# A Mamba layer on one core: roots and statistics moved to ScalarE, gates of two blocks in one instruction, and a new plan of parts

## The chip, the core and the metric

The kernel runs on one core of one Trainium2 chip. The core has five engines that run side by side, each taking its own instructions in order: TensorE (PE in the profile, with its weight loads shown as PEld), VectorE (DVE), ScalarE (ACT), GpSimd (POOL) and SyncE (SP), which here issues all DMA transfers. They meet through semaphores. SBUF is the working memory of 128 partitions; PSUM takes what PE computes[...]. The metric is the device time in microseconds of one execution, taken as the median of several runs.

## The reference, cut to what matters

The input x has 4 images of 384 channels and 64 x 64 pixels. Two layers follow each other, each with a group norm (32 groups of 12 channels) in front and the input added behind.

```python
# layer 0: a Mamba block over the L = 4096 pixels of each image
xn = (xs - mu) * rsqrt(var + 1e-5) * ln_w + ln_b        # over channels, of the group-normed x
xb, z = split(xn @ in_proj.T)                           # 768 and 768
xc = silu(conv4(xb) + conv_b)
dt, Bm, Cm = split(xc @ x_proj.T)                       # 24, 16, 16
dt = softplus(dt @ dt_w.T + dt_b)
h = exp(dt * A) * h + (dt * xc) * Bm                    # a scan over L, 768 x 16 states
y = sum_n(h * Cm) + xc * D
x1 = x + (y * silu(z)) @ out_proj.T
# layer 1: outlook attention on the group-normed x1, windows of 3 x 3, stride 2
out = x1 + proj(fold(softmax(attn(pool(g(x1)))) @ values(g(x1))))
```

The group norm in front of layer 1 needs mean and variance of x1 for each group of 12 channels, over all 4096 pixels of an image. All numbers are fp32.

## The kernel before, in words

**Tiling.** The pixels of each image are cut into 17 chunks of 241 (the first has 240 of its own and one column of zeros), 68 chunks in all. Channel 3p + cb lies in partition p, so a group of 12 channels is 4 partitions times NCB = 3 column blocks, and `blk12`, a matrix with blocks of 4 x 4, averages over a group on PE.

**The scan.** A chunk's 768 x 16 states are done in 12 steps, each a *unit* of two half-units (k = 0, 1) of 128 x 968 numbers. A step costs:
- `s_inputs` (L625) on POOL and `s_inputs2` (L640) on DVE: the products dt * x * B for one half each of the states, written into the tile h (five buffers, L137). The trace shows them as h<-dxr,bc and h<-dxr,bp.
- `s_decay` (L649) on ScalarE: eight ACTIVATEs exp(dt * A) into two PSUM tiles da, one per half (da<-dtr,aneg).
- `s_scan` (L661) on DVE: two scan instructions (h<-da,h).
- `s_outputs` (L671) on POOL: h times C in place (h<-h,bc).
- every second step `s_sum` (L676) on PE: 17 matmuls sum the states of two units into the PSUM tile y; then `s_gate` (L694) on DVE multiplies y by silu(z) (zs<-y,zs).
- two small copies on ScalarE, `s_carry` and `s_save`, that hand the last state on.

In step s of the main loop (L805) the engines are at different units: DVE scans unit s, ScalarE makes the decays of s + 1, POOL multiplies s - 1 by C and then makes the inputs of s + 2, PE sums s - 3 and s - 2, DVE gates s - 3.

**The parts.** All else of a chunk is cut into parts, functions that issue one or a few instructions. The dictionary `plan` (L506) says at which step, and at which of six places within the step (EARLY, READY, SCAN, POOL, MID, LATE), each part stands; the step is counted so that a chunk's units are scanned in steps 24 to 35, and a chunk begins every 12 steps. So a place at step 18 is met at step 6 of every twelve. `ends` (L540) is the same for the part behind the scan, counted from step 36. This hand-written order is final: the wrapper InOrder keeps each engine's instructions in the order of issue, so an instruction that waits holds everything behind it on its engine.
- `f_load` to `f_scale` (the layer norm): x in; mean by PE; center on DVE; square on ScalarE; variance by PE; `f_root` (L316) adds 1e-5 on DVE; `f_pow` (L321) raises to -0.5 on POOL (vs<-vs,mhalf); `f_rs` spreads it by PE; scale on DVE.
- `f_x`, `f_z`, `f_conv`, `f_silu`, `f_bc`, `f_xd`, `f_dt`: projections, convolution, silu (two table loads around it on ScalarE) and the small projections.
- `f_plog` (L482), `f_dtx` (L487): Ln(1 + exp) on ScalarE into PSUM (ps_lg), times xc on DVE (dtx), stored to DRAM by four DMAs; `f_log` does the same Ln into SBUF and stores it; `f_spread` loads B and C over the partitions; `f_b` makes PE's copy of B (bp).
- `e_load`, `e_project` (L710), `e_store` (L718): x again; out_proj plus x on PE, copied by ScalarE (xr<-ps_out); three bn_stats on DVE for the group norm of layer 1, and the store of x1.

All these PSUM results but y, da and bp share the pool `pmm` (L139) with two buffers: the third user waits until the first is read.

**Group norm.** `group_norm_coeffs` (L76) turns bn_stats into scale and bias; it runs in pieces between steps. The statistics of the next image's x are gathered on the way, two instructions per chunk (x_stat, L823) in 12 chunks of each of the first three images.

While the last chunks are scanned, the first tile of layer 1 begins (from L851). Layer 1 has its own loop and the change does not touch it.

Of the kernel before, what the change touches and what calls it, by code (L numbers as in the profile page):

```python
# [12 lines left out]
P = 128  # L13
# [59 lines left out]
        self.before = group[:-1]  # L73


def group_norm_coeffs(pe, ve, ae, gp, small, psum, blk12, mhalf, st, sc, bi):  # L76

    mv = small.tile([P, NCB, 2], F32, tag="mv", name="mv")  # L80
    neg = small.tile([P, 1], F32, tag="mg", name="neg")
    dev = small.tile([P, NCB], F32, tag="dev", name="dev")
    for cb in range(NCB):
        ve.bn_aggr(mv[:, cb, :], st[cb])
    yield False
    ps = psum.tile([P, 2, TM], F32, tag="mm", name="pm")
    for cb in range(NCB):
        pe.matmul(ps[:, 0, 0:1], blk12, mv[:, cb, 0:1], start=(cb == 0), stop=(cb == NCB - 1))
    yield True
    ae.mul(neg, ps[:, 0, 0:1], -1.0)  # L90
    ae.activation(dev, mv[:, :, 0], AF.Square, bias=neg)
    yield False
    ps = psum.tile([P, 2, TM], F32, tag="mm", name="pv")
    for cb in range(NCB):
        pe.matmul(ps[:, 0, 0:1], blk12, mv[:, cb, 1:2], start=(cb == 0), stop=False)
    for cb in range(NCB):
        pe.matmul(ps[:, 0, 0:1], blk12, dev[:, cb : cb + 1], start=False, stop=(cb == NCB - 1))
# [8 lines left out]
def mamba_layer(ctx, tc, x, w, x1, sc1, bi1, consts, behind):  # L106
# [13 lines left out]

    nc = tc.nc
    B, _, L = x.shape
    blk12, ident, eps, one = consts
    pe, ve, ae, gp, sp = (
        InOrder(tc, e) for e in (nc.tensor, nc.vector, nc.scalar, nc.gpsimd, nc.sync)
    )
# [19 lines left out]
        sp.dma_start(t, w[name])  # L146
        return t

    mhalf = wp.tile([P, 2], F32, tag="mhalf", name="mhalf")
    gp.memset(mhalf, -0.5)  # L150


# [163 lines left out]
    def f_root(c):  # L316
        n = c.spans[0][1]
        c.vs = front.tile([P, 2], F32, tag="vs", name="vs")
        ve.tensor_scalar_add(c.vs[:n, :], c.pv[:n, :, 0], 1e-5)

    def f_pow(c):  # L321
        n = c.spans[0][1]
        gp.tensor_tensor(c.vs[:n, :], c.vs[:n, :], mhalf[:n, :], ALU.pow)

    def f_rs(c):
        c.ps = pmm.tile([P, 2, TM], F32, tag="mm", name="ps_rs")
# [172 lines left out]
    def at(f, *args):  # L499
        def part(c):  # L500
            f(c, *args)

        part.f = f
        return part

    plan = {  # L506
        (-12, SCAN): [f_load],
        (-10, EARLY): [f_mean],
        (-10, READY): [f_center],
        (-9, LATE): [f_square],  # L510
        (-7, EARLY): [f_var],
        (-7, MID): [f_root],
        (-6, LATE): [f_pow],
        (-5, READY): [f_rs],
        (-5, SCAN): [f_scale],
        (6, LATE): [at(f_x, 0)],
        (8, EARLY): [at(f_z, 0)],
        (8, MID): [at(f_x, 1)],
        (9, POOL): [at(f_z, 1)],
        (9, LATE): [at(f_conv, 0)],  # L520
        (10, LATE): [at(f_z, 2)],
        (11, LATE): [at(f_x, 2)],
        (12, MID): [at(f_conv, 1)],
        (13, SCAN): [at(f_conv, 2)],
        (13, POOL): [at(f_silu, "xc", "zs")],
        (14, POOL): [f_bc],
        (15, EARLY): [f_xd],
        (16, READY): [at(f_dt, 0)],
        (16, SCAN): [at(f_dt, 1)],
        (16, MID): [at(f_dt, 2)],  # L530
        (17, READY): [at(f_plog, 0)],
        (17, MID): [at(f_dtx, 0)],
        (18, EARLY): [at(f_plog, 1)],
        (18, SCAN): [at(f_dtx, 1), at(f_plog, 2)],
        (19, EARLY): [at(f_dtx, 2)],
        (19, MID): [f_log, f_spread],
        (22, SCAN): [f_b],
    }
# [137 lines left out]
    def s_sum(u, u2):  # L676

        c, t = u.c, u.t
        y = py.tile([P, TM], F32, tag="y", name="y")
        pe.matmul(y[:, :t], ddiag[:, u.j, :], c.xc[:, u.j, :TM], start=True, stop=False, skip_group_check=True)  # L680
        for g in range(NG):
            for i in range(4):
                h4 = (u, u2)[i // 2].h4
                pe.matmul(
                    y[CG * i : CG * (i + 1), :t],
                    ssum,
                    h4[:, i % 2, g, :TM],
                    start=False,
                    stop=(g == NG - 1),
                    skip_group_check=True,  # L690
                )
        u2.y = y

    def s_gate(u):  # L694
        c, t = u.c, u.t
        ve.tensor_mul(c.zs[:, u.j, :t], u.y[:, :t], c.zs[:, u.j, :t])


    st1 = {}
# [10 lines left out]
    def e_project(c, cb):  # L710
        lo = c.lo
        po = pmm.tile([P, 2, TM], F32, tag="mm", name="ps_out")
        pe.matmul(po[:, 0, lo:], ident, c.xr[:, cb, lo:TM], start=True, stop=False)
        for j in range(NJ):
            pe.matmul(po[:, 0, lo:], wout[:, j, cb, :], c.zs[:, j, lo:TM], start=False, stop=(j == NJ - 1))
        ae.copy(c.xr[:, cb, lo:TM], po[:, 0, lo:])

    def e_store(c):  # L718
        if c.ci == 0:
            st1[c.b] = small.tile([P, NCB, NC, 6], F32, tag="st1", name="st1")  # L720
        for cb in range(NCB):
            ve.bn_stats(st1[c.b][:, cb, c.ci, :], c.xr[:, cb, c.lo : TM])
        sp.dma_start(e_tokens(c, x1), c.xr[:, :, c.lo : TM])
        if c.ci == NC - 1:
            b = c.b
            st = [st1[b][:, cb].rearrange("p a s -> p (a s)") for cb in range(NCB)]
            made = group_norm_coeffs(
                pe, ve, ae, gp, small, pmm, blk12, mhalf, st, sc1[:, b : b + 1], bi1[:, b : b + 1]
            )
            norms.append([made, False])  # L730

# [73 lines left out]
    for s in range(-4, NU * (len(chunks) + 2)):  # L805
        k, m = divmod(s, NU)
        if m % 2 == 0 and unit(s + 4) is not None:
            s_fetch(s + 4)
        parts(s, EARLY)
        if m % 4 == 3 or s >= NU * len(chunks):  # L810
            norm_part(False)

        if (u := unit(s + 1)) is not None:
            s_inputs2(u)
        if (u := unit(s - 3)) is not None and not u.first:
# [12 lines left out]
        for i in range(2):  # L828
            if (u := unit(s)) is not None:
                s_scan(u, i)  # L830
            if i == 1:
                parts(s, SCAN)
            if (u := unit(s + 1)) is not None:
                if i == 0:
                    s_carry(u)
                s_decay(u, i)
            if i == 0 and (u := unit(s - 1)) is not None:
                s_save(u)
        if (u := unit(s - 1)) is not None:
            s_outputs(u)  # L840
        norm_part(True)
        parts(s, POOL)
        if (u := unit(s + 2)) is not None:
            s_inputs(u)
        if (u := unit(s - 2)) is not None and not u.first:
            s_sum(unit(s - 3), u)
        parts(s, MID)
        parts(s, LATE)
        if s == front_end:
            fronts.close()  # L850
        if s >= front_end:  # L851
            over = das[0] if s >= NU * len(chunks) - 1 else None
            behind(lambda: pmm.tile([P, 2, TM], F32, tag="mm", name="psv").rearrange("p a b -> p (a b)"), over)
# [386 lines left out]
def layers(ctx, tc, w, out):  # L1240
# [5 lines left out]
    x1 = dram.tile([B, C, H * W], F32, tag="x1", name="x1")  # L1246
    blk12 = cp.tile([P, P], F32, tag="blk12", name="blk12")
    nc.sync.dma_start(blk12, w["blk12"])
    ident = cp.tile([P, P], F32, tag="ident", name="ident")
    nc.sync.dma_start(ident, w["ident"])  # L1250
    eps = cp.tile([P, 1], F32, tag="eps", name="eps")
# [5 lines left out]
    consts = (blk12, ident, eps, one)  # L1257
    weights, ready = {}, []
    later = outlook_before(ctx, tc, w, x1, H, W, sc1, bi1, dram, weights, ready)

# [12 lines left out]
def layouts(inputs):  # L1273
# [38 lines left out]
    a["ident"] = np.eye(P, dtype=f)  # L1312
    a["avg"] = np.full((P, P), 1.0 / C, f)
    a["blk12"] = np.kron(np.eye(P // 4, dtype=f), np.full((4, 4), 1.0 / 12.0, f)).astype(f)
    a["onesc"] = np.full((P, 1), 1.0 / C, f)
    r = np.arange(P)
    k = np.arange(P)
# [22 lines left out]
```

## Time and profile before

| | |
|---|---|
| median of 3 runs | 6228.52 us (6228.22 to 6234.19) |
| the profiled execution | 6226.19 us, its span 6224.4 us |
| mean granted TensorE clock | 0.941 |
| POOL multiplies the first and the last unit by C | from 116.9 to 4994.5 us |
| ACT_TABLE_LOAD | 137, 1283 ns each |

The span is the time from the first to the last instruction of one profiled execution. A group of the profile reads: line, engine, operation, result<-operands, shapes, count, then the busy time and the mean of one in ns, then the idle time just before and what ended it. Every line is L49, the call in InOrder, so groups are told apart by the names of their tiles. In the slices, each digit is the busy tenth of a fortieth of the span. An instruction may begin before the one in front of it on its engine has ended, so a group's mean is a little more than what one costs in a row of several.

### The profile page before, as it was taken

How to read it: one execution, taken by the hardware profiler on the slowest of the kernel's cores; microseconds unless marked ns; L12 is line 12 of the kernel's file. 1: busy time of each engine (PE TensorE's matmuls, PEld its weight loads, DVE VectorE, ACT ScalarE, POOL GpSimd, SP SyncE). 2: the span in 40 equal slices, each digit the busy share in tenths (PEclk: the TensorE clock that was granted, in tenths of full speed). 3: DMA queues.
4: the chain of work that ended last, by engine and by line, in shares of the span. 5: the costliest groups of instructions: out<-in, count | busy, mean ns of one | idle time of the engine just before them, and what ended most of it. 6: DMA issues, size and time to landing. Idle time of an engine off the chain costs nothing. (4 is left out here: it accounts for less than half of the span.)

```text
span 6224.4 us, 114423 instructions
## 1 busy us (share of the span) xinstructions
PE 5485.2 (88%) x40506; PEld 4055.1 (65%) x40506; DVE 5363.2 (86%) x4786; ACT 4667.1 (75%) x11842; POOL 5307.3 (85%) x2047
## 2 busy tenths in 40 slices
PE   6888888888888888888888888888888789999999
PEld 5666666666666666666666666666666455555555
DVE  4999999999999999999999999999999954454444
ACT  3788888888888888888888888888888744444544
POOL 3999999999999999999999999999999944333334
PEclk9999999999999999999999999999999899999999
DMA  4555555555555555545555544455455644444544
GB/s 134 131 139 146 149 137 136 133 135 143 147 136 141 140 133 143 144 131 141 141 139 148 141 126 133 133 144 139 129 133 132 176 138 168 168 166 171 171 168 149
DMA packets 649764, 894.94 MB, mean 144 GB/s; under 512 B 138964, under 2 KB 543846, under 8 KB 649062
## 3 DMA queue, kind: packets, MB, share of 16 engines
q1 hardware_dynamic: 649190, 887.63, 51.3%
q8 instruction: 319, 5.23, 0.4%
q14 instruction: 255, 2.09, 0.1%
HBM read 661.53 MB, written 225.70 MB: 143 GB/s over the span
## 5 line engine op out<-in xcount | busy, mean ns | idle before, releaser
L49 DVE TENSOR_TENSOR_SCAN h<-da,h 128x968 f32<-128x968 f32 x1632 | 3451.6, 2157 | 47.5 <-POOL h L49 23.4
L49 POOL TENSOR_TENSOR h<-h,bc 128x1928 f32<-128x1928 f32 x816 | 3227.7, 3956 | 10.4 <-DVE h L49 10.4
L49 ACT ACTIVATE da<-dtr,aneg 128x241 f32<-128x241 f32 x6528 | 2642.7, 451 | 490.4 <-DVE h L49 452.5
L49 POOL TENSOR_TENSOR h<-dxr,bc 128x964 f32<-128x964 f32 x816 | 1626.3, 1993 | 70.0 <-PE y L49 47.3
L49 PE MATMUL ps_in<-u,win 128*128 128x241 f32 x4896 | 1073.5, 373 | 45.0 <-DVE dtx L49 33.5
L49 PEld LDWEIGHTS ps_in<-u,win 128*128 128x128 f32 x4896 | 910.9, 190 | 202.3 <-ACT zs L49 32.8
L49 POOL TENSOR_TENSOR bd<-ain,own 99x1188 f32<-99x1188 f32 x192 | 413.5, 2181 | 726.6 <-DMA ain<-ad 554.6
L49 DVE TENSOR_TENSOR h<-dxr,bp 128x964 f32<-128x964 f32 x816 | 928.9, 1138 | 22.6 <-PE y L49 13.7
L49 PE MATMUL y<-h,ssum 128*32 128x241 f32 x13056 | 862.9, 389 | 46.9 <-POOL h L49 46.9
L49 PE MATMUL ps_cv<-xb,cdiag 128*128 128x241 f32 x3264 | 693.9, 368 | 5.7 <-ACT neg L49 5.5
L49 PEld LDWEIGHTS y<-h,ssum 128*32 128x32 f32 x13056 | 427.1, 114 | 409.0 <-issue 155.6
L49 PEld LDWEIGHTS ps_cv<-xb,cdiag 128*128 128x128 f32 x3264 | 611.0, 189 | 78.2 <-issue 25.9
L49 PE MATMUL psv<-wv,xp 128*128 128x384 f32 x1728 | 592.7, 495 | 7.0 <-issue 7.0
L49 PE MATMUL ps_xd<-xc,wx 128*128 128x241 f32 x816 | 309.0, 558 | 323.9 <-ACT xc L49 323.9
L49 PE MATMUL ps_out<-zs,wout 128*128 128x241 f32 (+1 forms) x2448 | 592.0, 396 | 0.0
L49 PEld LDWEIGHTS ps_out<-zs,wout 128*128 128x128 f32 x2448 | 510.2, 208 | 50.7
L49 ACT ACTIVATE bd<-ain,own 99x324 f32<-99x324 f32 x704 | 334.5, 555 | 262.8 <-PE ps L49 241.3
L49 DVE TENSOR_TENSOR fold<-fold,ps 128x192 f32<-128x192 f32 (+1 forms) x768 | 211.0, 303 | 332.6 <-PE ps L49 318.2
L49 PEld LDWEIGHTS ps_xd<-xc,wx 128*128 128x128 f32 x816 | 241.8, 306 | 388.1 <-ACT xc L49 349.3
L49 PEld LDWEIGHTS psv<-wv,xp 128*128 128x128 f32 x1728 | 322.6, 191 | 232.1 <-issue 19.4
L49 ACT COPY vst<-psv 128x384 f32<-128x384 f32 x279 | 130.8, 469 | 323.5 <-PE psv L49 323.5
L49 PE MATMUL ps_dt<-xd,wdt 128*128 128x241 f32 x816 | 205.9, 389 | 71.7 <-ACT dt L49 64.6
(108 smaller groups left out, 5410.2 us busy)
## 6 DMA issues: line engine op xcount, KB each, us to landing
dxr<-dxd SPq DMA_DIRECT2D x1632, 120.5 KB
dtr<-dtd SPq DMA_DIRECT2D x1632, 120.5 KB
bc<-bcd SPq DMA_DIRECT2D x544, 120.5 KB
vin<-vd SPq DMA_DIRECT2D x384, 148.5 KB
vd<-vst SPq DMA_DIRECT2D x93, 576.0 KB
dxd<-dtx SPq DMA_DIRECT2D x816, 60.2 KB
dtd<-dt SPq DMA_DIRECT2D x272, 180.8 KB
xs<-in_x SPq DMA_DIRECT2D x96, 256.0 KB
```

The costliest lines, as they stand in the source:

```text
L49: made = self.tc.keep_in_program_order(issue(*args, **kwargs))
```

## The change

- `f_root` becomes Ln(var + 1e-5) and `f_pow` becomes Exp(-0.5 * that), both on ScalarE.
- `e_project`'s copy on ScalarE becomes an Identity that also accumulates each row's sum (`accum_out`); a new part `e_mean` adds the three sums into a mean, and `e_store` squares the deviations on ScalarE and accumulates them. A record of (count, mean, sum of squares) replaces three bn_stats; `group_norm_coeffs` takes one record list in place of three, with `blk4`, whose weights are 1/4.
- y holds two blocks j, and `s_gate` runs every fourth step for both.
- Most parts of `plan` and `ends` stand at other places.

```diff
     def f_root(c):
-        ve.tensor_scalar_add(c.vs[:n, :], c.pv[:n, :, 0], 1e-5)
+        ae.activation(c.vs[:n, :], c.pv[:n, :, 0], AF.Ln, bias=eps[:n, :])
     def f_pow(c):
-        gp.tensor_tensor(c.vs[:n, :], c.vs[:n, :], mhalf[:n, :], ALU.pow)
+        ae.activation(c.vs[:n, :], c.vs[:n, :], AF.Exp, scale=-0.5)
...
     plan = {
-        (-10, EARLY): [f_mean],
-        (-10, READY): [f_center],
-        (-9, LATE): [f_square],
-        (-7, EARLY): [f_var],
-        (-7, MID): [f_root],
-        (-6, LATE): [f_pow],
-        (-5, READY): [f_rs],
-        (-5, SCAN): [f_scale],
-        (6, LATE): [at(f_x, 0)],
+        (-11, LATE): [f_mean],
+        (-9, READY): [f_center],
+        (-9, SCAN): [f_square],
+        (-7, READY): [f_var],
+        (-7, SCAN): [f_root],
+        (-6, READY): [f_pow],
+        (-6, POOL): [f_rs],
+        (-5, POOL): [f_scale],
+        (7, LATE): [at(f_x, 0)],
         (8, EARLY): [at(f_z, 0)],
         (8, MID): [at(f_x, 1)],
-        (9, POOL): [at(f_z, 1)],
         (9, LATE): [at(f_conv, 0)],
-        (10, LATE): [at(f_z, 2)],
+        (10, SCAN): [at(f_z, 1)],
+        (10, POOL): [at(f_z, 2)],
         (11, LATE): [at(f_x, 2)],
-        (12, MID): [at(f_conv, 1)],
+        (13, READY): [at(f_conv, 1)],
         (13, SCAN): [at(f_conv, 2)],
         (13, POOL): [at(f_silu, "xc", "zs")],
-        (14, POOL): [f_bc],
-        (15, EARLY): [f_xd],
-        (16, READY): [at(f_dt, 0)],
-        (16, SCAN): [at(f_dt, 1)],
-        (16, MID): [at(f_dt, 2)],
+        (14, EARLY): [f_bc],
+        (15, SCAN): [f_xd],
+        (16, SCAN): [at(f_dt, 0), at(f_dt, 1)],
+        (16, LATE): [at(f_dt, 2)],
         (17, READY): [at(f_plog, 0)],
-        (17, MID): [at(f_dtx, 0)],
+        (17, POOL): [at(f_dtx, 0)],
         (18, EARLY): [at(f_plog, 1)],
-        (18, SCAN): [at(f_dtx, 1), at(f_plog, 2)],
-        (19, EARLY): [at(f_dtx, 2)],
-        (19, MID): [f_log, f_spread],
+        (18, READY): [at(f_plog, 2), at(f_dtx, 1)],
+        (18, POOL): [at(f_dtx, 2)],
+        (19, SCAN): [f_spread],
+        (19, MID): [f_log],
     ends = {
-        (-9, READY): [lambda c: e_load(c)],
+        (-12, LATE): [lambda c: e_load(c)],
         (4, READY): [lambda c: e_project(c, 0)],
         (6, EARLY): [lambda c: e_project(c, 1)],
-        (6, POOL): [lambda c: e_project(c, 2)],
-        (14, POOL): [lambda c: e_store(c)],
+        (6, SCAN): [lambda c: e_project(c, 2)],
+        (7, READY): [lambda c: e_mean(c)],
+        (7, LATE): [lambda c: e_store(c)],
...
     def s_sum(u, u2):
-        y = py.tile([P, TM], F32, tag="y", name="y")
+        if u.j % 2 == 0:
+            c.y = py.tile([P, 2, TM], F32, tag="y", name="y")
+        y = c.y[:, u.j % 2]
     def s_gate(u):
-        ve.tensor_mul(c.zs[:, u.j, :t], u.y[:, :t], c.zs[:, u.j, :t])
+        ve.tensor_mul(c.zs[:, j : j + 2, :t], c.y[:, :, :t], c.zs[:, j : j + 2, :t])
...
     def e_project(c, cb):
-        ae.copy(c.xr[:, cb, lo:TM], po[:, 0, lo:])
+        ae.activation(c.xr[:, cb, lo:TM], po[:, 0, lo:], AF.Identity, accum_out=c.sums[:, cb : cb + 1])
+    def e_mean(c):
+        ae.activation(c.sums, c.sums, AF.Identity, scale=1.0 / (NCB * n), accum_out=st1[c.b][:, c.ci, 1:2])
     def e_store(c):
-        for cb in range(NCB):
-            ve.bn_stats(st1[c.b][:, cb, c.ci, :], c.xr[:, cb, c.lo : TM])
+        ae.activation(
+            c.zs[:, :NCB, :n], c.xr[:, :, c.lo : TM], AF.Square,
+            scale=-1.0, bias=st1[c.b][:, c.ci, 1:2], accum_out=st1[c.b][:, c.ci, 2:3],
+        )
```

More of the change, by code (lines that the diff above doesn't have):

```diff
@@ L73, in apart, with group_norm_coeffs @@
         self.before = group[:-1]
-def group_norm_coeffs(pe, ve, ae, gp, small, psum, blk12, mhalf, st, sc, bi):
+def group_norm_coeffs(pe, ve, ae, gp, small, psum, blk, mhalf, st, sc, bi):
+    n = len(st)
     mv = small.tile([P, NCB, 2], F32, tag="mv", name="mv")
@@ L82, in group_norm_coeffs @@
     dev = small.tile([P, NCB], F32, tag="dev", name="dev")
-    for cb in range(NCB):
+    for cb in range(n):
         ve.bn_aggr(mv[:, cb, :], st[cb])
@@ L86, in group_norm_coeffs @@
     ps = psum.tile([P, 2, TM], F32, tag="mm", name="pm")
-    for cb in range(NCB):
-        pe.matmul(ps[:, 0, 0:1], blk12, mv[:, cb, 0:1], start=(cb == 0), stop=(cb == NCB - 1))
+    for cb in range(n):
+        pe.matmul(ps[:, 0, 0:1], blk, mv[:, cb, 0:1], start=(cb == 0), stop=(cb == n - 1))
     yield True
     ae.mul(neg, ps[:, 0, 0:1], -1.0)
-    ae.activation(dev, mv[:, :, 0], AF.Square, bias=neg)
+    ae.activation(dev[:, :n], mv[:, :n, 0], AF.Square, bias=neg)
     yield False
     ps = psum.tile([P, 2, TM], F32, tag="mm", name="pv")
[L94 to L97, printed above, removed]
+    for cb in range(n):
+        pe.matmul(ps[:, 0, 0:1], blk, mv[:, cb, 1:2], start=(cb == 0), stop=False)
+    for cb in range(n):
+        pe.matmul(ps[:, 0, 0:1], blk, dev[:, cb : cb + 1], start=False, stop=(cb == n - 1))
     yield True
@@ L122, in mamba_layer @@
     B, _, L = x.shape
-    blk12, ident, eps, one = consts
+    blk12, blk4, ident, eps, one = consts
     pe, ve, ae, gp, sp = (
@@ L147, in load @@
         return t
-    mhalf = wp.tile([P, 2], F32, tag="mhalf", name="mhalf")
+    mhalf = wp.tile([P, 1], F32, tag="mhalf", name="mhalf")
     gp.memset(mhalf, -0.5)
@@ L691, in s_sum @@
                 )
-        u2.y = y
     def s_gate(u):
-        c, t = u.c, u.t
-        ve.tensor_mul(c.zs[:, u.j, :t], u.y[:, :t], c.zs[:, u.j, :t])
+        c, t, j = u.c, u.t, u.j - 1
+        ve.tensor_mul(c.zs[:, j : j + 2, :t], c.y[:, :, :t], c.zs[:, j : j + 2, :t])
     st1 = {}
@@ L715, in e_project @@
             pe.matmul(po[:, 0, lo:], wout[:, j, cb, :], c.zs[:, j, lo:TM], start=False, stop=(j == NJ - 1))
-        ae.copy(c.xr[:, cb, lo:TM], po[:, 0, lo:])
-    def e_store(c):
-        if c.ci == 0:
-            st1[c.b] = small.tile([P, NCB, NC, 6], F32, tag="st1", name="st1")
-        for cb in range(NCB):
-            ve.bn_stats(st1[c.b][:, cb, c.ci, :], c.xr[:, cb, c.lo : TM])
+        if cb == 0:
+            c.sums = small.tile([P, NCB], F32, tag="sums", name="sums")
+        ae.activation(c.xr[:, cb, lo:TM], po[:, 0, lo:], AF.Identity, accum_out=c.sums[:, cb : cb + 1])
+    def e_mean(c):
+        n = TM - c.lo
+        if c.ci == 0:
+            st1[c.b] = small.tile([P, NC, 3], F32, tag="st1", name="st1")
+            gp.memset(st1[c.b][:, 0:1, 0:1], float(NCB * n))
+            gp.memset(st1[c.b][:, 1:, 0:1], float(NCB * TM))
+        ae.activation(
+            c.sums,
+            c.sums,
+            AF.Identity,
+            scale=1.0 / (NCB * n),
+            accum_out=st1[c.b][:, c.ci, 1:2],
+        )
+    def e_store(c):
+        n = TM - c.lo
+        ae.activation(
+            c.zs[:, :NCB, :n],
+            c.xr[:, :, c.lo : TM],
+            AF.Square,
+            scale=-1.0,
+            bias=st1[c.b][:, c.ci, 1:2],
+            accum_out=st1[c.b][:, c.ci, 2:3],
+        )
         sp.dma_start(e_tokens(c, x1), c.xr[:, :, c.lo : TM])
@@ L725, in e_store @@
             b = c.b
-            st = [st1[b][:, cb].rearrange("p a s -> p (a s)") for cb in range(NCB)]
             made = group_norm_coeffs(
-                pe, ve, ae, gp, small, pmm, blk12, mhalf, st, sc1[:, b : b + 1], bi1[:, b : b + 1]
+                pe, ve, ae, gp, small, pmm, blk4, mhalf, [st1[b].rearrange("p a s -> p (a s)")], sc1[:, b : b + 1], bi1[:, b : b + 1]
             )
@@ L814, in mamba_layer @@
             s_inputs2(u)
-        if (u := unit(s - 3)) is not None and not u.first:
+        if (u := unit(s - 3)) is not None and not u.first and u.j % 2:
             s_gate(u)
@@ L1248, in layers @@
     nc.sync.dma_start(blk12, w["blk12"])
+    blk4 = cp.tile([P, P], F32, tag="blk4", name="blk4")
+    nc.sync.dma_start(blk4, w["blk4"])
     ident = cp.tile([P, P], F32, tag="ident", name="ident")
@@ L1256, in layers @@
     bi1 = cp.tile([P, B], F32, tag="bi1", name="bi1")
-    consts = (blk12, ident, eps, one)
+    consts = (blk12, blk4, ident, eps, one)
     weights, ready = {}, []
@@ L1314, in layouts @@
     a["blk12"] = np.kron(np.eye(P // 4, dtype=f), np.full((4, 4), 1.0 / 12.0, f)).astype(f)
+    a["blk4"] = np.kron(np.eye(P // 4, dtype=f), np.full((4, 4), 0.25, f)).astype(f)
     a["onesc"] = np.full((P, 1), 1.0 / C, f)
```

## The prediction

> **What bounds the kernel now.** I began with the page: how full each engine is, and when.
>
> ```profile
> span 6224.4 us, 114423 instructions
> PE 5485.2 (88%) x40506; PEld 4055.1 (65%) x40506; DVE 5363.2 (86%) x4786; ACT 4667.1 (75%) x11842; POOL 5307.3 (85%) x2047
> DVE  4999999999999999999999999999999954454444
> POOL 3999999999999999999999999999999944333334
> ```
>
> For 31 of 40 slices, the first layer, DVE and POOL are both full; later neither is. The windows, by stretch, separate them (busy PE, PEld, DVE, ACT, POOL):
>
> ```profile
> 2000.00:3000.00 1000.00, 869.63 (x5826) 682.69 (x5828) 974.24 (x742) 832.22 (x2181) 988.63 (x354) 0.93 0.53 139
> 4500.00:4900.00 400.00, 331.77 (x2236) 257.95 (x2232) 385.53 (x285) 334.97 (x875) 398.08 (x141) 0.93 0.50 129
> ```
>
> POOL is 98.9% busy in the middle and 99.5% in the last batch; ScalarE has 17% left. Then the groups, with shapes kept apart, give what each does:
>
> ```profile
> L49 POOL TENSOR_TENSOR h<-h,bc 128x1928 f32<-128x1928 f32 x816 | 3227.7, 3956 | 10.4 <-DVE h L49 10.4
> L49 POOL TENSOR_TENSOR h<-dxr,bc 128x964 f32<-128x964 f32 x816 | 1626.3, 1993 | 70.0 <-PE y L49 47.3 <-DMA dxr<-dxd 11.3 <-ACT st L49 5.7
> L49 POOL TENSOR_TENSOR vs<-vs,mhalf 121x2 f32<-121x2 f32 x68 | 47.9, 705 | 39.4 <-DVE vs L49 39.4
> L49 DVE BATCH_NORM_STATS2 st<-xr 128x6 f32<-128x241 f32 x192 | 64.6, 394 | 0.0
> ```
>
> Last, the timeline of one chunk, steps 5 to 7 of its twelve (start, duration, engine, instruction, idle before it):
>
> ```profile
> 3031.30 3.95 POOL L49 TENSOR_TENSOR h<-h,bc 128x1928 f32<-128x1928 f32 x1
> 3034.14 0.36 ACT L49 COPY xr<-ps_out 128x241 f32<-128x241 f32 x1 [3.54 <-PE ps_out L49]
> 3035.20 1.99 POOL L49 TENSOR_TENSOR h<-dxr,bc 128x964 f32<-128x964 f32 x1
> ...
> 3036.84 0.66 DVE L49 TENSOR_TENSOR dtx<-ps_lg,xc 128x482 f32<-128x482 f32 x1 [1.79 <-ACT ps_lg L49]
> 3037.15 0.69 POOL L49 TENSOR_TENSOR vs<-vs,mhalf 121x2 f32<-121x2 f32 x1
> ...
> 3037.65 2.69 PE L49 MATMUL ps_in<-u,win 128*128 128x241 f32 x12
> 3037.80 3.96 POOL L49 TENSOR_TENSOR h<-h,bc 128x1928 f32<-128x1928 f32 x1
> 3041.12 1.84 PE L49 MATMUL y<-h,ssum 128*32 128x241 f32 x32
> 3043.12 1.98 POOL L49 TENSOR_TENSOR h<-dxr,bc 128x964 f32<-128x964 f32 x1 [1.36 <-PE y L49]
> ```
>
> Instructions on one engine overlap by some 0.06 to 0.1 us, so I count from start to start where nothing waits: POOL 3.90, 1.94 and, for the power, 0.65. **POOL's floor** for a chunk is 12 x (3.90 + 1.94) + 0.65 = 70.73 us. I took the starts of every twelfth h<-h,bc in the timeline: 67 periods, the first 91.4 (start-up), the other 66 together 4717.9 us. The 36 with statistics of the next batch's x (two x_stat each) have a mean of 71.6, 27 without 71.1, and three at a batch's border 73.8. The fastest take 70.73: bare POOL. The rest, about 0.7, is POOL waiting, in 46 of 63 steady chunks at the place above: s_inputs (L625) needs the h buffer that s_sum (L676) reads, one of five, and PE comes to that sum late, behind f_x's projection and f_rs's transpose. These are late because two dtx (L487) and three projections pass the two PSUM buffers of pmm (L139) hand over hand, in the order of ScalarE.
>
> **DVE's own sum**, start to start in a chunk with statistics: 24 scans x 2.073 + 12 products x 1.054 + 6 gates x 0.32 + 3 dtx x 0.57 + 3 bn_stats x 0.31 + center 0.875 + scale 0.86 + root 0.05 + 2 x_stat x 0.60 = 69.9. In the traces its stalls come to about 1.24 (second and third dtx wait for ps_lg) and 0.4 (below): 71.5, as measured. So DVE sets chunks with statistics, POOL the others.
>
> **The change, part by part (per chunk).**
>
> *f_pow off POOL:* one instruction, -0.65 on POOL. Its floor becomes 70.07.
>
> *f_root off DVE:* -0.05; *three bn_stats off DVE:* 3 x 0.31 = -0.92; *six gates to three:* 482 columns from PSUM and SBUF are the shape of dtx, so 3 x 0.57 for 6 x 0.32, -0.21. DVE's work is 68.8 with statistics, 67.6 without.
>
> *Added on ScalarE:* Ln and Exp of 121x2, near the 8-column copies (0.19 each, twice 0.19); Square over 723 columns, as sq (0.88); e_mean of three columns, about 0.2. Together 1.5. New is the accumulated column, five per chunk, which no row shows. Below: free. Above: the page VectorE: DVE Perf Modes of the Trainium skill (Two Vector instructions with no wait between them) says of VectorE that an operation which writes its accumulator is two instructions; if ScalarE did likewise, each costs another copy of 0.09 start to start up to 0.19 whole, 0.5 to 0.95. I take 0.5. ScalarE's idle time was about 11.9 per chunk (17%), so 2.0 fits, if it doesn't sit where a scan waits.
>
> *Table sets.* In the trace a table load starts at 2502.93 and the next ACTIVATE at 2504.22, 1.29 later. ScalarE: Activation LUTs of the Trainium skill (What ACT_TABLE_LOAD costs) asks about 2.66 us for each switch of set, 1.28 of it the load. Had Ln and Exp another set than the decays, two switches per chunk would be 68 x 2 x 1.29 = 175 us by the row, 362 by the page. The changed program has 137 loads, as before, so I add none.
>
> *Where ScalarE's work sits.* da has one buffer per half, so a decay (4 x 0.39) runs only between the scan that frees it and the next one of its half. Silu with two loads, 5.4 us, is the one long block already there:
>
> ```profile
> 2506.93 1.28 ACT L49 ACT_TABLE_LOAD   x1
> 2508.33 1.62 ACT L49 ACTIVATE da<-dtr,aneg 128x241 f32<-128x241 f32 x4
> 2510.03 2.17 DVE L49 TENSOR_TENSOR_SCAN h<-da,h 128x968 f32<-128x968 f32 x1 [0.70 <-POOL h L49]
> ```
>
> (The releaser named had long been done; the decay ended at 9.95.) bn_stats had filled 0.92 of this gap, so taking them away gives time back here: counted from the end of the scan two before, that scan could start at 7.7 (gate 0.57, product 1.05, scans 4.15, product 1.05, center 0.875), the decay is ready at 9.0 (2500.95 to 2509.95). Stall 1.3, or 0.7 where an x_stat of 0.60 fills it. A second block arises at step 8: dt's Ln 1.39, xb's two copies 0.65, Square 0.8, two zs 0.7, with accumulation 3.7; the decay behind it ends about 7.3 after the last scan (decay 1.65, block 3.7, carry 0.1, decay 1.65, and 0.2 for Square's wait on the mean) and DVE is there at 7.1. I take a stall of 0.3. Ln of the root and sq stand between two decays, where the decay may start 1.4 later unpunished.
>
> *dtx and ps_lg at new places.* dtx 1 now stands behind the product and gate of step 18, about 2.2 after the scan; its ps_lg ends at 2.3 to 2.5. dtx 2 stands behind the next two scans, when its ps_lg has long ended, even behind an xr copy that waits 3.5 for PE. Stall 0.2 instead of 1.24.
>
> *f_x behind s_sum.* PE reaches the sum without the 2.6 of ps_in x12, and without the power; POOL's wait there (0.64 per chunk) goes. f_x's readers, xb then f_conv, come a step later: xb waits behind dt's Ln anyway.
>
> *The other parts moved* (f_mean, f_center, f_square, f_var, f_bc, f_conv, f_z) stay ahead of their readers; PE idles 9.3 per chunk, 4.8 of it for silu, in both. f_mean now holds one pmm buffer from step 1 to 3, where f_bc alone wants another. bp (f_b) stands behind 2.6 more of f_z on PE and can keep DVE 1.0 when that is a whole step ahead of POOL; then it costs nothing.
>
> *DMAs and queues.* f_spread's eight loads now stand in front of f_log's four stores on SP; these wait for dt's Ln as before. e_store's one store comes seven steps earlier, behind f_log's; it delays the fetch of step 8 by its 0.58 issue. f_xd's copies come about 3 later, and SP holds its two stores and then the fetch of step 4 for that; POOL needs that fetch two steps on (11.7), and SP issues its eight parts in 4.4, so it stays covered by about 4 less the landing; uncovered it would be POOL's wait one for one. e_load is earlier. Nothing enters the path.
>
> *Sum.* DVE with statistics 68.8 + 0.7 + 0.2 + 0.3 = 70.0, without 69.4; POOL 70.07. POOL binds, by a hair in the first kind. I add 0.23 for that hair: 70.3 (36 chunks), 70.15 (27), and 72.0 at borders, where two of three bn_aggr (0.49 each) go too. Gain 36 x 1.3 + 27 x 0.9 + 3 x 1.8 = 77. Start-up loses about 1.5: ScalarE stands at 92.4 with f_root of the third chunk, whose variance PE ends at 93.7, and three ps_lg queue behind. The end: bn_stats and two bn_aggr go, but the pixels behind wait for a load (5.0 idle), so 0. Span 6224.4 - 75.5 = 6148.9. The profiled execution took 6226.19, 1.8 over its span, and the median of three is 2.3 above that: 6228.5 - 75.5 = **6153**.
>
> **Rivals.**
>
> *Only the power is gained* (POOL goes on waiting for late sums, or DVE for ps_lg): 66 x 0.65 = 43, 6185. For it: coupled waits tend to reappear, and DVE and POOL are within 0.1. Against: in the last batch POOL mostly ran at its bare floor of 70.73 with DVE's sum and stalls at 69.9 - 1.2 + 1.64 = 70.3.
>
> *Slower: ScalarE becomes the bound at steps 8 and 3.* If an accumulated column or its wait (Square's bias is the mean that e_mean has just written) costs far more, the block of step 8 grows and each microsecond is DVE's, as in silu's gap. From 70.0 to 71.5 is 1.5: beyond 1.5 more per chunk it decides; at 2.5 DVE takes 72.5 in chunks with statistics and 71.9 in others, 36 x 0.9 + 27 x 0.8 = 54 slower, 6282. Against: that is 0.5 us for each of five columns, over twice a whole copy.
>
> *Nothing:* stalls eat all that is saved: 6228.
>
> **How the numbers follow.** POOL-bound as summed 0.76 (own range 6137 to 6173: the bare floor in every chunk is 36 x 1.54 + 27 x 1.0 + 3 x 2.5 = 90 below the time before; 0.3 more stall in each of 66 chunks is 20 above the sum); only the power 0.12; nothing 0.03; slower 0.09. The measurement tells 0.2%, 12 us, from no change. Faster 0.88, same 0.03, slower 0.09. The range runs from 6134 (the bare floor, with start-up 3 better than counted) through the power-only case to 6188.
>
> **What would show it.** Right: POOL's periods at 70.1 to 70.4, its wait for PE y near nothing, its power gone; DVE under 98% busy, dtx's wait under 0.3 per chunk, the scan behind silu waiting 0.7 to 1.3; Square about 0.9. Wrong: DVE's scans wait for da at step 8 by more than 1; an extra ScalarE instruction of several tenths behind each accumulated column; POOL's sums late again.

## The result, and the profile after

The changed kernel takes 6229.18 us (median of 12 runs, 6204.24 to 6240.72), the kernel before, run beside it, 6230.04 us (12 runs, 6228.0 to 6236.25). The ratio is 0.9994, with a 95% interval of [0.9983, 1.0005]: no difference, where the prediction had a gain of 75.5 us. The profiled execution took 6232.9 us. Of all runs named below, one of the kernel with f_xd put back is left out, which took 13700.6 us at a granted clock of 0.41.

From the page of the changed kernel, the span, the engines, and two rows of the slices and the granted clock:

```profile
span 6231.1 us, 114471 instructions
PE 5542.2 (89%) x40458; PEld 4081.3 (65%) x40458; DVE 5280.4 (85%) x4302; ACT 4753.6 (76%) x12454; POOL 5262.7 (84%) x1987
DVE  3999999999999999999999999999999954454444
POOL 3999999999999999999999999999999944333334
PEclk9899999999989899999899999999899899999999
```

DVE has 83 us less to do and POOL 45, as the change intends, and the span is 7 longer. The same two windows as before (busy PE, PEld, DVE, ACT, POOL, then clock, DMA share, GB/s):

```profile
2000.00:3000.00 1000.00, 880.90 (x5795) 686.31 (x5796) 953.68 (x639) 847.60 (x2300) 976.48 (x341) 0.91 0.52 138
4500.00:4900.00 400.00, 344.73 (x2287) 266.91 (x2286) 377.85 (x246) 339.69 (x921) 393.94 (x137) 0.90 0.49 129
```

POOL was full (988.63 of 1000); now it, too, has slack, and so have DVE and ScalarE. No engine is full: they wait for each other. PE's clock fell from 0.93 to 0.91 and to 0.90. The groups of the changed kernel say for whom POOL and DVE wait:

```profile
L49 POOL TENSOR_TENSOR h<-h,bc 128x1928 f32<-128x1928 f32 x816 | 3230.2, 3959 | 6.2 <-DVE h L49 4.7 <-DMA dxr<-dxd 1.5
L49 POOL TENSOR_TENSOR h<-dxr,bc 128x964 f32<-128x964 f32 x816 | 1626.0, 1993 | 160.0 <-PE y L49 91.3 <-DMA dxr<-dxd 54.0 <-ACT ps_lg L49 7.1
L49 DVE TENSOR_TENSOR h<-dxr,bp 128x964 f32<-128x964 f32 x816 | 926.5, 1136 | 130.3 <-PE y L49 121.6 <-DMA dxr<-dxd 8.7
L49 PE MATMUL ps_dt<-xd,wdt 128*128 128x241 f32 x816 | 236.1, 418 | 127.8 <-ACT dt L49 92.9 <-ACT xr L49 30.0 <-ACT xd L49 3.2
L49 ACT ACTIVATION_READ_ACCUMULATOR xr<-ps_out 128x1 f32 x204 | 39.5, 194 | 0.0
```

Before, POOL's second line had 70.0 of idle time, 47.3 for y, and DVE's product this:

```profile
L49 DVE TENSOR_TENSOR h<-dxr,bp 128x964 f32<-128x964 f32 x816 | 928.9, 1138 | 22.6 <-PE y L49 13.7 <-DMA dxr<-dxd 8.3
```

(The 54.0 for dxr lie in the first 200 us.) So sums of y are late, but not where they were. Before, POOL waited at step 7, for the sum behind f_x and the root's transpose; that wait is gone. The new one is a sum earlier, at step 5, where y is summed for the chunk's units 2 and 3: in 54 of 63 steady chunks (here and below the fourth to the 66th of the 68), 1.25 us per chunk on POOL, 1.67 for the DVE product that reuses an h buffer of the same sum. Steps 4 and 5 of a chunk of the changed kernel, from the timeline (start, duration, engine, instruction, idle before):

```profile
3093.40 0.35 ACT L49 COPY xd<-ps_xd 56x241 f32<-56x241 f32 x1
...
3093.81 1.08 PE L49 MATMUL ps_dt<-xd,wdt 128*128 128x241 f32 x4 [0.17 <-ACT xd L49]
...
3095.71 1.08 PE L49 MATMUL ps_dt<-xd,wdt 128*128 128x241 f32 x4 [0.82 <-ACT xr L49]
3095.94 1.62 ACT L49 ACTIVATE da<-dtr,aneg 128x241 f32<-128x241 f32 x4 [0.18 <-DVE h L49]
...
3097.59 1.01 ACT L49 ACTIVATE dt<-ps_dt 128x482 f32<-128x482 f32 x2
...
3098.20 1.98 PE L49 MATMUL ps_dt<-xd,wdt 128*128 128x241 f32 x4 [1.41 <-ACT dt L49]
...
3099.97 2.45 PE L49 MATMUL ps_var<-onesc,sq 128*121 128x1 f32 x12
3100.15 3.96 POOL L49 TENSOR_TENSOR h<-h,bc 128x1928 f32<-128x1928 f32 x1
...
3102.28 1.15 PE L49 MATMUL y<-xc,ddiag 128*128 128x241 f32 x2
...
3103.36 3.44 PE L49 MATMUL y<-h,ssum 128*32 128x241 f32 x32
...
3106.84 1.16 DVE L49 TENSOR_TENSOR h<-dxr,bp 128x964 f32<-128x964 f32 x1 [3.13 <-PE y L49]
3106.98 1.98 POOL L49 TENSOR_TENSOR h<-dxr,bc 128x964 f32<-128x964 f32 x1 [2.87 <-PE y L49]
```

Two things are to be seen. **Order:** f_xd's copy now stands behind the decays and the square of step 3, and two of f_dt's exps stand behind the decay of 3095.94, so PE comes late to the three dt projections and stands idle twice between them (0.82 until an xr copy on ScalarE is done, 1.41 until dt's exp is), with the variance and the sum queued behind. **Clock:** after that idle time the very same instructions take about twice as long: 1.98 against 1.08, the sum 3.44. In the record of the granted clock PE has only two levels, full and half, in stretches of 3.41 us or multiples, all on one grid that runs through the whole execution.

The same steps of the kernel before, another chunk, from its timeline:

```profile
3020.63 1.89 PE L49 MATMUL ps_dt<-xd,wdt 128*128 128x241 f32 x8 [1.17 <-ACT dt L49]
...
3023.40 1.43 PE L49 MATMUL ps_var<-onesc,sq 128*121 128x1 f32 x12 [0.87 <-ACT dt L49]
...
3025.28 2.60 PE L49 MATMUL y<-h,ssum 128*32 128x241 f32 x32
...
3029.36 2.00 POOL L49 TENSOR_TENSOR h<-dxr,bc 128x964 f32<-128x964 f32 x1
```

Here the sum ends at 3027.88 and POOL comes for it at 3029.36. In the changed kernel's chunk it ends at 3106.80, and POOL was ready at 3104.11. At full clock it would, by this estimate, have come in time: the four pieces from the third dt projection to the sum take 1.08 and 1.43 at full clock, as shown, and 0.57 and 1.84, as y's two groups take in an undisturbed step. That is 0.90 + 1.02 + 0.58 + 1.60 = 4.1 us less, an end at 3102.7.

### The profile page after: what moved, and what is told of

The parts are those of the page before. It is cut to its first block, busy times and chain, and to the rows that moved or that the text cites. A ratio compares the mean times of both kernels' runs of the same rounds, so it can differ in the third digit from the quotient of the medians.

```text
span 6231.1 us, 114471 instructions
## 1 busy us (share of the span) xinstructions
PE 5542.2 (89%) x40458; PEld 4081.3 (65%) x40458; DVE 5280.4 (85%) x4302; ACT 4753.6 (76%) x12454; POOL 5262.7 (84%) x1987
## 4 chain that ended last, share of the span: by engine, by line
DVE 32%; PE 27%; ACT 16%; POOL 8%; issue 6%; DMA 6%; SPq 4%; DVEq 0%; POOLq 0%; ACTq 0%
DVE h L49 29%; ACT da L49 11%; PE psv L49 9%; POOL h L49 8%; SPq L49 4%; PE pso L49 4%; PE ps L49 3%; PE y L49 3%; PE psa L49 3%; DMA dxr<-dxd 2%; PE ps_out L49 2%; ACT dt L49 2%; DMA dtr<-dtd 1%; DVE dtx L49 1%; PE ps_var L49 1%
## 5 line engine op out<-in xcount | busy, mean ns | idle before, releaser
L49 PE MATMUL ps_in<-u,win 128*128 128x241 f32 x4896 | 1091.4, 373 | 37.4 <-DVE u L49 18.0
L49 PE MATMUL y<-h,ssum 128*32 128x241 f32 x13056 | 848.4, 403 | 32.5 <-POOL h L49 32.5
L49 PEld LDWEIGHTS y<-h,ssum 128*32 128x32 f32 x13056 | 411.6, 118 | 418.8 <-issue 200.2
L49 PE MATMUL ps_xd<-xc,wx 128*128 128x241 f32 x816 | 331.4, 591 | 330.7 <-ACT xc L49 330.7
L49 PE MATMUL ps_out<-zs,wout 128*128 128x241 f32 (+1 forms) x2448 | 541.1, 370 | 0.0
L49 PEld LDWEIGHTS ps_xd<-xc,wx 128*128 128x128 f32 x816 | 254.6, 322 | 399.0 <-ACT xc L49 356.1
L49 PEld LDWEIGHTS ps_out<-zs,wout 128*128 128x128 f32 x2448 | 475.3, 194 | 39.1
L49 PE MATMUL ps_dt<-xd,wdt 128*128 128x241 f32 x816 | 236.1, 418 | 127.8 <-ACT dt L49 92.9
```

Source lines behind the costliest of these rows:

```text
L49: made = self.tc.keep_in_program_order(issue(*args, **kwargs))
```

## The experiments

I took as theory after this reading that f_xd's and f_dt's new places are the whole loss. In the tables that follow, *wait* is POOL's wait for y at step 5 per chunk over the 63 steady chunks, and *half clock* is the time per chunk for which PE's granted clock was half (before: wait 0.05, half clock 9.5 us; changed kernel: 1.25 and 12.6).

**Both parts at their old places.** The kernel as changed, but:

```diff
-        (15, SCAN): [f_xd],
-        (16, SCAN): [at(f_dt, 0), at(f_dt, 1)],
-        (16, LATE): [at(f_dt, 2)],
+        (15, EARLY): [f_xd],
+        (16, READY): [at(f_dt, 0)],
+        (16, SCAN): [at(f_dt, 1)],
+        (16, MID): [at(f_dt, 2)],
```

> The changed kernel with four parts (f_xd and the three f_dt) back at the places of the kernel before; all else as changed. Theory (the sum of step 5 is late on PE, because f_xd's copies and the dt projections, which stand before it, come about 3 us later and wait for ScalarE): POOL's wait for PE y at the sum of step 5, 1.25 us per chunk in the changed kernel, falls under 0.3, the share of half clock falls towards that of before, and the time is about 6160 (6140 to 6185). Rival (the added work on ScalarE is what holds DVE, at the scan behind silu and at step 8): nothing much changes, 6210 to 6235.

Measured: 6145.98 us (6143.81 to 6146.78), ratio 0.9863 [0.9848, 0.9878]. The wait is 0.00 and half clock 6.6. It beats both kernels, and lies 7 us from the predicted time. Its window 2000:3000:

```profile
2000.00:3000.00 1000.00, 886.17 (x5966) 692.17 (x5965) 976.84 (x653) 868.24 (x2350) 998.68 (x350) 0.95 0.54 142
```

And from its timeline the two lines of a chunk's step 5 that answer to those above:

```profile
3043.47 1.84 PE L49 MATMUL y<-h,ssum 128*32 128x241 f32 x32
...
3048.94 1.96 POOL L49 TENSOR_TENSOR h<-dxr,bc 128x964 f32<-128x964 f32 x1
```

POOL is 99.9% busy, and the sum ends 3.6 us before POOL comes for what it frees. All of the loss is in these three lines of the plan.

**One of the two parts at a time.** Only the line of f_xd is put back, then only those of f_dt.

> The changed kernel with f_xd alone back at step 15 EARLY (its two copies on ScalarE in front of a decay instead of behind the square); the f_dt stay at the new places. Theory (the late copies of xd start the delay; the dt projections only follow them): most of the gain of the four parts together, 6155 to 6180, and half clock at step 5 below 0.4. Rival (the order of the dt projections, with none ahead of the first out projection and two behind one another waiting for ScalarE, makes PE idle and late): little changes, 6205 to 6230.

> The changed kernel with the three f_dt alone back at their old places; f_xd stays at step 15 SCAN. Theory (late xd): the first dt projection still waits for xd, and the out projection now behind it on PE waits too, 6200 to 6230. Rival (the order of the dt projections): most of the gain, 6155 to 6180.

| f_xd | f_dt | us | ratio | wait |
|---|---|---|---|---|
| new | new | 6229.18 | 0.9994 [0.9983, 1.0005] | 1.25 |
| old | new | 6234.69 | 1.0006 [0.9997, 1.0015] | 1.32 |
| new | old | 6257.02 | 1.0043 [1.0028, 1.0058] | 1.49 |
| old | old | 6145.98 | 0.9863 [0.9848, 0.9878] | 0.00 |

Neither does it alone, and I had expected f_xd's place to bring nearly all. The second time lies above both of the ranges that I had put. With f_xd early, PE's dt projections still stand behind the first out projection, and the third waits for an exp behind a decay. With f_dt early they stand ahead of the out projection, and the first waits for the late xd, with everything behind it. From the timeline of the kernel with f_xd back, the third dt projection:

```profile
3029.76 1.08 PE L49 MATMUL ps_dt<-xd,wdt 128*128 128x241 f32 x4 [1.88 <-ACT dt L49]
```

And from that of the kernel with f_dt back, the first:

```profile
3034.72 1.08 PE L49 MATMUL ps_dt<-xd,wdt 128*128 128x241 f32 x4 [2.34 <-ACT xd L49]
```

In both, PE idles and the sum comes late; only with both parts early does that end. In the kernel with f_dt back the order does this without more half clock: 9.8 us of it per chunk, about as before (9.5), and a wait of 1.49.

**The change in two halves.** First the kernel of before (f_root, f_pow, bn_stats and the gates on their old engines) with the whole plan and ends of the changed one, less e_mean, which it doesn't have:

```diff
-        (7, READY): [lambda c: e_mean(c)],
```

Then the changed kernel's parts at the places of before, where e_mean and e_store alone stand as in the change:

```diff
-        (14, POOL): [lambda c: e_store(c)],
+        (7, READY): [lambda c: e_mean(c)],
+        (7, LATE): [lambda c: e_store(c)],
```

> The kernel before with the new plan of parts alone: roots on DVE and POOL, bn_stats and single gates as before. Theory (the new plan costs what the moved work saves): 0.65 of the power and 1.2 of late sums per chunk on POOL over its floor of 70.07, about 72.2 per chunk, 6250 to 6285. Rival (ScalarE's added work is what eats the gain): the new plan without that work is no slower than before, 6190 to 6230.

> The changed kernel with the old plan of parts (e_mean at step 7 READY and e_store at step 7 LATE, as they must stand in front of the next use of zs): the moved work without the moved parts. Theory (the moved work saves, the plan costs): DVE about 68.8 of work with statistics, 1.24 of waits for ps_lg and 1.0 behind silu, so about 71.0, and without statistics POOL at 70.1 to 70.5: 6180 (6160 to 6205). Rival (ScalarE's added work eats the gain): 6215 or more.

The first took 6305.81 us, ratio 1.0116 [1.0101, 1.0131], wait 1.55, more than either theory had. So the plan by itself costs 1.2%, and the moves of work would then have to be worth as much. But the second took 6288.51, ratio 1.0094 [1.0079, 1.0109]: with the old places the moved work costs 0.9%, where a gain was expected. That is the rival's range, and it is work added on ScalarE, at its old place, that the timeline shows at the start of the waits:

```profile
2992.18 0.24 ACT L49 ACTIVATE vs<-ps_var,eps 121x2 f32<-121x2 f32 x1
...
2992.48 1.17 PE L49 MATMUL ps_out<-xr,ident 128*128 128x241 f32 x2 [3.03 <-ACT vs L49]
...
2997.28 0.37 ACT L49 ACTIVATE xr<-ps_out 128x241 f32<-128x241 f32 x1 [4.30 <-PE ps_out L49]
...
3000.07 0.66 DVE L49 TENSOR_TENSOR dtx<-ps_lg,xc 128x482 f32<-128x482 f32 x1 [2.60 <-ACT ps_lg L49]
...
3006.29 1.98 POOL L49 TENSOR_TENSOR h<-dxr,bc 128x964 f32<-128x964 f32 x1 [2.38 <-PE y L49]
```

The root on ScalarE stands behind a decay, and until it has read ps_var one of the two buffers of pmm is held. PE waits 3.03 for it, and 1.17 where 0.67 is usual shows half clock again. Then ScalarE, DVE and POOL wait in turn. PE's wait for this root stands in 62 of the 63 chunks, 2.44 us per chunk; with the new places and f_xd and f_dt back it is 0.47. No run moved the root alone, so its share of the loss is read from the traces and not tested. The new engines need new places; of those, f_xd's and f_dt's cost what all the rest brought.

**Order or clock?** In the changed kernel both come together. Needless matmuls of 15 columns ahead of the second and third dt projection leave every other instruction where it is and keep PE from idling there. My first attempt wrote them into spare columns of bp:

```diff
-    bp = pbb.tile([P, 2, TM], F32, tag="bp", name="bp")
+    bp = pbb.tile([P, 2, 256], F32, tag="bp", name="bp")
...
+    def keep_warm(n):
+        for _ in range(n):
+            pe.matmul(bp[:, 1, TM:256], ident, ident[:, : 256 - TM], start=True, stop=True)
...
+        if jj:
+            keep_warm((0, 4, 6)[jj])
         pp = pmm.tile([P, 2, TM], F32, tag="mm", name="ps_dt")
```

> The changed kernel with 4 and 6 needless matmuls of 15 columns (into columns of bp that nobody reads) in front of the second and the third dt projection, where PE idles 1.8 us per chunk; order of all else unchanged. Theory A (these idle times bring the half clock, and the half clock makes the variance and the sum late): half clock at steps 4 and 5 nearly goes, POOL's wait for PE y goes with it, about 6165. Theory B (the order alone makes the sum late): the sum starts as late as before, POOL still waits about 1 us per chunk, 6215 to 6235.

It took 6189.51 us, ratio 0.9939 [0.9923, 0.9956], wait 0.55, between the two theories. But DVE's products read bp, and now waited for the needless matmuls as well (32.5 us for PE bp over the run), though they read none of those columns. So I wrote them into spare columns of the y tile that is being filled (live_y), which DVE reads only after another sum has followed:

```diff
-            c.y = py.tile([P, 2, TM], F32, tag="y", name="y")
+            c.y = live_y[0] = py.tile([P, 2, 256], F32, tag="y", name="y")
...
-            pe.matmul(bp[:, 1, TM:256], ident, ident[:, : 256 - TM], start=True, stop=True)
+            pe.matmul(live_y[0][:, 1, TM:256], ident, ident[:, : 256 - TM], start=True, stop=True, skip_group_check=True)
```

> As the changed kernel, but PE runs 4 and 6 needless matmuls of 15 columns ahead of the second and third dt projection, where it waited 1.8 us per chunk for ScalarE's exps; unlike the earlier attempt they write columns of the y tile that nobody reads, and not columns of bp. The theory that the half clock, which follows PE's waiting, makes a large part of what lateness costs expects half clock at step 5 below 0.25 (from 0.64), no new wait of a DVE product, and 6155 to 6185. The rival, that the order of the dt projections alone makes the sum of step 5 late and the clock is a bystander, expects half clock gone but POOL still waiting about 1 us per chunk for y, and 6200 to 6230.

It took 6182.57 us, ratio 0.9924 [0.9907, 0.994], and 6192.0 where it was profiled; half clock at step 5, from its scan to the next, fell from a share of 0.62 to 0.28, not below 0.25, and the wait to 0.63. The time is inside the range of the clock theory, at its upper end, and its half clock is above what that theory expected. The chunks of this one kernel tell them apart better than its median: whether a chunk is struck depends mostly on where it falls on the clock's grid, and the instructions are the same. Two such chunks, each from the scan of step 3 on, in the windows view of this kernel:

```profile
720.00:738.00 18.00, 17.75 (x122) 13.65 (x124) 15.19 (x9) 16.93 (x48) 16.43 (x6) 0.78 0.29 82
793.00:811.00 18.00, 17.61 (x142) 14.23 (x141) 17.11 (x12) 16.93 (x48) 18.00 (x7) 0.94 0.30 81
```

With the clock at 0.78 PE gets 122 matmuls done in 18 us of its time and POOL idles 1.6; with 0.94 it gets 142 done and POOL is full. Sorted over all 63 chunks by PE's time at half clock from step 4 to 3 us into step 6, and with the *room*, the time from the end of y's sum to POOL's coming for it, both from the timelines:

| | chunks under 0.5 us | wait | room | chunks over 5 us | wait | room |
|---|---|---|---|---|---|---|
| before | 6 | 0.00 | 3.45 | 17 | 0.17 | 1.33 |
| changed | 5 | 0.10 | 1.09 | 41 | 1.72 | -1.54 |
| needless matmuls in y | 36 | 0.00 | 2.05 | 21 | 1.90 | -1.73 |
| both parts at old places | 27 | 0.00 | 3.16 | 1 | 0.29 | -0.14 |

Sorting is not an experiment, since a late chunk might bring half clock on itself. But in the kernel with needless matmuls the struck chunks (over 5 us) and those under 0.5 us begin their first dt projection alike, 4.6 and 4.7 us ahead of POOL's inputs of step 4, and their sums end 7.6 and 3.9 us behind that point. They part after the dt projections have begun, so an earlier lateness does not explain the sorting. The grid does: 19 of the 21 struck chunks, and 3 of the 36 others, begin that projection 2.05 to 2.7 us into one of the clock's windows of 3.41 us.

So in the changed kernel it takes both. The new order takes about 2.4 us of the room (3.45 to 1.09, the latter from five chunks only), which at full clock is still enough. Half clock takes another 2.1 to 3.8, which before there was room for. And the new order brings more half clock to this place, 41 chunks over 5 us where there were 17. In the 36 undisturbed chunks of the kernel with needless matmuls the period is 70.19 us, 0.12 over POOL's bare floor: with the clock up, the new order costs next to nothing there.

**The clock at silu.** PE waits 4.9 us per chunk for silu, and the half clock after that wait (step 2, share 0.77) lies ahead of all this. Needless matmuls ahead of f_bc were tried there too: in bp, on the changed kernel and on the one with the old places, and then in f_bc's own PSUM tile.

```diff
         px = pmm.tile([P, 2, TM], F32, tag="mm", name="ps_xd")
+        for _ in range(18):
+            pe.matmul(px[:, 1, :15], ident, ident[:, :15], start=True, stop=True)
```

> The changed kernel with 18 needless matmuls of 15 columns on PE in its wait for silu, in front of f_bc: the half clock that follows this wait at step 2 (0.77 of the step) goes, and ps_xd runs at full speed. Theory (only the half clock at steps 4 and 5 counts, as xd waits for ScalarE's order and not for PE): time within 15 us of the changed kernel, 6215 to 6240. Rival (any half clock before the sums counts): about 6180 or less.

> The changed kernel with the four parts at their old places, and the needless matmuls in the wait for silu. Theory (with these places POOL's own work, 70.07 per chunk, is the bound, and the clock of PE no longer counts): the granted clock rises towards 0.97 and the time stays at 6146 within 6 us. Rival (PE still sets some of the chunks): 6125 to 6138.

> As the changed kernel, but PE runs 18 needless matmuls of 15 columns ahead of the B/C/dt projection, where it waits 4.8 us for silu, into columns of that projection's own PSUM tile that nobody reads. The half clock of step 2 (share 0.77, before 0.72, in the version with the old places 0.53) lies ahead of everything that comes late at step 5. If it matters, the xd copies come 1 us earlier, POOL's wait for y at step 5 halves, and the time is 6170 to 6200. The rival, that xd's place in ScalarE's queue sets it whatever PE's clock, expects 6220 to 6240. If the PSUM buffer isn't free early, the needless matmuls only delay the projection, and the time is above 6240.

> Both sets of needless matmuls in the changed kernel. The clock theory expects clock above 0.96, POOL's wait for y under 0.3 us per chunk and 6145 to 6170, as with the old places; the order theory expects 6190 or more.

The first two took 6462.14 us (1.0374 [1.0359, 1.039]) and 6351.05 (1.0185 [1.0162, 1.0209]). DVE's products waited 281.5 and 276.6 us for PE bp, some 4 us per chunk, so they tell nothing of the clock. The third, in which DVE waits for none of them, took 6229.0 us, 0.9996 [0.9986, 1.0006], as the rival had it. PE's idle time ahead of f_bc fell from 4.9 to 0.7 us per chunk, yet the share of half clock at step 2 only from 0.77 to 0.66. Being busy by the profile with such short matmuls did not release the clock here, so whether a full clock at silu would help was not tested. Both sets together took 6181.0 us, 0.9921 [0.9905, 0.9936], no better than those at dt alone, though half clock at step 5 fell to 0.20 and the wait to 0.22. The clock theory had expected a clock above 0.96 and 6145 to 6170; POOL's wait came out as it said, the clock (0.949 to 0.955) and the time did not. The order theory's 6190 or more did not come either. The trace shows a new wait: POOL stands 0.28 per chunk at step 3 for an earlier sum of y, in 15 of the 63 chunks. With the set ahead of f_bc alone that wait is 0.18, with the set at dt alone it is 0, so it comes with the set ahead of f_bc. It and the 0.22 at step 5 are nearly all by which the mean period, 70.74, exceeds that with both parts at their old places, 70.21; and POOL's first product starts at 126.6, there at 118.3. So this kernel is no clean test of a full clock.

## Why the prediction was wrong, step by step

- **POOL without the power, 70.07 as its floor: right.** With the two parts back, 36 chunks with statistics have a mean period of 70.10, and 27 without 70.20.
- **DVE's work: right.** The two-block gate takes 0.57 from start to start, as put; bn_stats and root are gone.
- **ScalarE's additions: right.** Square takes 0.80 from start to start, Ln 0.195, Exp 0.094, and the table loads stay 137. The accumulated column is a second instruction, as weighed by the row of the copies. The group shown above has it: 194 ns whole, 0.093 from start to start, so about 0.5 for five.
- **Silu's gap: the mechanism right, the size a little low.** The scan of step 3 waits 0.98 in 34 chunks with an x_stat there (0.7 put), and 1.50 in 28 without (1.3 put). The chunk shown above has:

```profile
3088.53 4.24 DVE L49 TENSOR_TENSOR_SCAN h<-da,h 128x968 f32<-128x968 f32 x2 [0.97 <-POOL h L49]
```

- **Step 8, a stall of 0.3: not there,** at most 0.06 per chunk. The slower rival, ScalarE as the bound at steps 8 and 3, didn't happen.
- **dtx and ps_lg: right.** dtx's wait fell from 1.24 to 0.06 (0.2 put).
- **"f_x behind s_sum ... POOL's wait there goes": right** for that sum, at step 7.
- **"f_xd's copies come about 3 later ... Nothing enters the path": this step failed.** The copies do come later, by 3.7 (counted from POOL's inputs of step 4). I followed that along SP's queue and the fetches, and there it costs nothing, as POOL shows, which never waits for a DMA after the first 200 us. I didn't follow it along PE, where the dt projections read xd, and f_dt's own three places got no price at all. Behind them in PE's order stand the variance and the sum of step 5, which frees h buffers for POOL and DVE. The prediction traced the sum of step 7 in this manner, and took the sum of step 5, which didn't bind before, as safe.
- **PE's durations were taken as fixed: this is what made the loss a full one.** The prediction counted PE's idle time (9.3 per chunk) as slack. In the trace of before the two speeds could be read: y's sum in 2.60 where 1.84 is usual, an out projection in 4.11 where 2.61 is. A new idle place among PE's instructions can double the time of those behind it. In the few chunks at full clock the lateness cost POOL 0.10 us; in those with over 5 us of half clock, 1.72.
- **Start-up and end:** the first period fell by 1.2 where a loss of 1.5 was put, and with the old places it rose by 2.5.

The sum, then: the prediction had the 66 periods behind the first at 4717.9 - 77 = 4641 us. Without the failed step they are 4634.8; with it 4726.7. The rival "only the power is gained" named the right mechanism, POOL waiting for late sums, but took the wait as no larger than before, so it stood at 6185. The case "nothing" is what came.

## What to carry to other kernels

When a part is moved later, follow it along every engine that has instructions behind its readers, and most of all along the in-order engine whose result frees a buffer of the bound engine: a sum that doesn't bind yet has a room, which can be read from the timeline, and moves spend it. Read PE's durations at both of its clocks, and ask of each planned gap on PE what stands behind it, because that is what may run at half speed. And where several parts are moved together, an experiment with one put back can show nothing, as here, and two put back can show everything.

## What the hardware did that I had not expected

- PE's clock falls to half after windows with idle time in them, not only after empty ones. In the changed kernel PE was busy 0.43 and 0.61 of the 3.4 us ahead of such stretches in steps 4 and 5 on average, at most 0.73. The page TensorE: Matmul & The Clock Gate of the Trainium skill (Part 1) tells of a free-running window of 3413 ns and of two levels, half and full; the stretches in this trace, multiples of 3.41 us on a fixed grid, agree with it. I laid the steady chunks on that grid. In the changed kernel, windows at full clock that were followed by half clock had PE busy for 0 to 0.73 of their time, those followed by full clock for 0.52 to 1; in the kernel before it is 0 to 0.82 and 0.48 to 1. What decides between about 0.5 and 0.8 isn't settled by these runs.
- Matmuls of 15 columns hold the clock up less than the profile's busy time suggests. In the kernel with needless ones in y, windows busy up to 1.00 were followed by half clock, up to 0.80 when those matmuls aren't counted; and filling 4.2 us of PE's wait for silu with them left the clock at half nearly as often.
- The changed kernel's runs go with its clock: 6204.24 us at a mean of 0.935, 6221.6 at 0.929, 6240.7 at 0.924. Of its 66 chunk periods behind the first, 20 lie at 71.5 to 71.7 us (one before), and 21 windows of 3.413 are 71.68. It looks as if the chunks fall into step with the grid; I only saw this and didn't test it.
- Matmuls into columns of a PSUM tile that a reader doesn't touch still made that reader wait for them (DVE's products for the writes into bp's spare columns, up to 281.5 us). Here this comes with the kernel's semaphores, and whether the program or the hardware demands it wasn't tried.
